# Gathers issued two steps ahead into 22 buffers, and a block's maxima computed in three parts from one step sooner

## The chip, the cores and the metric

The kernel runs on one core of a Trainium2 chip. The metric is the device time of one execution in microseconds (us). The engines are named as in the profile: PE is TensorE, DVE is VectorE, ACT is ScalarE, POOL is GpSimd, and SP is SyncE, which here only issues transfers. PEld is PE's loading of weights.

## The reference

A graph layer with attention over relations, followed by a residual and two layer norms. There are 3125 nodes of 128 features, 100000 edges sorted by destination, five edge types (relations), and eight heads of 16 features. Cut to what matters:

```python
for r in range(R):                                   # 5 relations
    mask = edge_types == r
    q = einsum('eh,khd->ekd', x[dst], W_Q[r]); k = ...x[src], W_K[r]; v = ...x[src], W_V[r]
    logits = (q * k).sum(-1) / 4 + attn_bias[r]
    masked = where(mask, logits, -1e9)
    max_v = segment_max(masked, dst)                 # per node, relation, head
    exp_l = where(mask, exp(masked - max_v[dst]), 0)
    attn = exp_l / (segment_sum(exp_l, dst)[dst] + 1e-12)
    out += segment_sum(attn[:, :, None] * v, dst)
h = out @ out_proj_w.T + out_proj_b + x
y = x + layer_norm(h) * gamma + beta
result = layer_norm(y)
```

Every node therefore needs the largest logit of its edges, for each relation and head, before any of its edges can be weighted.

## The kernel before, in words

A first stage (until about 125 us in the profile) builds tables in HBM: keys and values of every node and relation (`kv_d`, 256 floats a row), queries (`q_d`), and indices of the edges.

The main stage is a software pipeline written out by hand. The edges are cut into 196 groups of 512, and the loop `for k in range(-4, ...)` is over *steps*. The order in which the calls stand in the loop is the order of each engine's instructions; every engine runs its own list in order and waits for others through semaphores. In step k these things happen, each on a group of its own:

- POOL gathers keys and values for a later group: `gather` (L699), four indirect transfers per group, into one of `KVB` buffers that are used in turn. A gather may start when the buffer's earlier group has been weighted (`weigh`, L939).
- PE spreads the maxima to the edges of a group that is due (`spread_m`, L921), sums weighted values (`sums`, L973, L975, L982), and spreads queries to the edges of the next group (`spread_q`, L804).
- DVE weights values (`weigh`, L939), subtracts maxima (`less_max`, L930), normalises a finished group (`norm`, L994 to L997), computes the logits of group k (`logits`: `prod` L817, `lg` L818), and marks destinations (`spot`, L795). There is one L817 per step, so these cut the trace into steps.
- ACT does exponentials, copies, and one-hot places (`places`, L959, L962). SP issues the other loads and stores, among them the logits' store to `lg_d` (L823).

The nodes are cut into 25 blocks of 128. A block needs its maxima once all of its edges have logits. Call F the step in which the last group that can hold an edge of the block has its logits (`full_step[b]` in the code; about every eighth step). Then:

- In step F+1, POOL loads the logits of the block's nodes, 64 edges for each, by one indirect transfer (`maxima_load`, L830, tile `ell`), behind that step's gather.
- In steps F+3 and F+4, at the end of DVE's list for the step, `maxima` finds the maxima: first `by_head` (ACT, L845) and `mine` (L853), then for each relation of the part a mask `shut` (L863), then for all of the part's relations at once a sum `wl` (L868) and a reduction into `mx` (L874). The first part takes three relations (`RH`), the second takes two, and ends with six small instructions that make three bfloat16 pieces (L879 to L889).
- In step F+5 the pieces are stored, in F+6 they are fetched for the first group of the block, and in step F+8 (`ready[b]`, `LAG` = 8) that group is weighted. The 25th block is smaller and does its maxima in one part.

Two other sequences share the engines with this. Every block's queries are made in steps of their own by PE (`queries`, L725, tile `prq`, one PSUM buffer), and the second product can start only after DVE's `remainder` (L735) has read the first. The finished nodes of a block pass through `project`, `residual`, `roots` and `norms`.

In the code, step F+3 is `ready[b] - 5` and F+4 is `ready[b] - 4`. A group is weighted 16 to 19 steps after its logits, 19 for all groups from number 22 on, counted from 0.

Of the kernel before, what the change touches and what calls it, by code (L numbers as in the profile page):

```python
# [21 lines left out]
R = 5  # L22
# [26 lines left out]
RH = 3  # L49
# [1 line left out]
LW = HEADS + 1  # L51
PW = H + HEADS
FAR = 4000
AHEAD = 3
LAG = 8
LAG_H = 7
HALVED = 0
# [3 lines left out]
SPAD = 5  # L61
XG = range(3, 16, 3)
QB = 3
KVB = 23
HELD = 21
KVA = 9

# [66 lines left out]
def windowed_path(  # L134
# [554 lines left out]
    ps = ctx.enter_context(tc.tile_pool(name="ps", bufs=2, space=PSUM))  # L689
    buffers(i for i in range(KVB) if i not in at_once)  # L690
    hold = ctx.enter_context(tc.tile_pool(name="hold", bufs=HELD))
    flow = ctx.enter_context(tc.tile_pool(name="flow", bufs=2))
    late_flow = ctx.enter_context(tc.tile_pool(name="late_flow", bufs=2))
    def gather(g):
        if g in XG:
            return
        kv = kvs_[g % KVB]
        for t in range(T):
# [61 lines left out]
    def turn_x(g):  # L760
        xe = kvs_[g % KVB][:, :, H:]
        tx = ps.tile([P, T, P], F32, name="tx", tag="me")
# [27 lines left out]
    def put_kv(g, t0):  # L790
        nc.scalar.copy(kvs_[g % KVB][:, t0 : t0 + 2, :], live.pop(("pk", g, t0)))

# [21 lines left out]
    def logits(g):  # L814
        kv, lg = kvs_[g % KVB], live["lg", g]
        prod = flow.tile([P, T, H], F32, name="prod", bufs=1)
# [20 lines left out]
    def maxima(b, c0, c1):  # L837

        whole = MB[b][2] is None
        nh = HEADS if whole else HEADS // 2  # L840
        if c0 == 0:
            ell = live.pop(("ell", b))
            by_head = ps.tile([P, HEADS, D], F32, name="by_head", bufs=1)[:, :nh]
            if whole:
                nc.scalar.copy(by_head, ell[:, :, :HEADS].rearrange("p s k -> p k s"))  # L845
            else:
                for h in range(2):
                    at = slice(h * P // 2, (h + 1) * P // 2)
                    nc.scalar.copy(
                        by_head[at], ell[at, :, h * nh : (h + 1) * nh].rearrange("p s k -> p k s")  # L850
                    )
            mine = late_flow.tile([P, D], F32, name="mine", bufs=1)
            nc.vector.scalar_tensor_tensor(  # L853
                mine, slot, deg[:, b : b + 1], ell[:, :, HEADS], op0=ALU.is_lt, op1=ALU.mult
            )
            mx = late_flow.tile([P, R, HEADS], F32, name="mx", bufs=1)
            mx = mx.rearrange("p r k -> p (r k)")[:, : R * nh].rearrange("p (r k) -> p r k", k=nh)
            live["max", b] = by_head, mine, mx
        by_head, mine, mx = live["max", b]
        n = c1 - c0  # L860
        shut = late_flow.tile([P, R, D], F32, name="shut", bufs=1)
        for r in range(c0, c1):
            nc.vector.tensor_scalar(  # L863
                shut[:, r - c0, :], mine, float(r + 1), -BIG, op0=ALU.not_equal, op1=ALU.mult
            )
        wl = late_flow.tile([P, RH * HEADS, D], F32, name="wl", tag="wl", bufs=1)
        wl = wl[:, : n * nh].rearrange("p (r k) s -> p r k s", k=nh)
        nc.vector.tensor_tensor(  # L868
            wl,
            by_head[:, None].to_broadcast([P, n, nh, D]),  # L870
            shut[:, :n, None, :].to_broadcast([P, n, nh, D]),
            op=ALU.add,
        )
        nc.vector.tensor_reduce(mx[:, c0:c1], wl, AX.X, ALU.max)  # L874
        if c1 < R:
            return
        live.pop(("max", b))
        bias = bias4 if whole else bias_h
        nc.vector.tensor_tensor(mx, mx, bias, op=ALU.add)  # L879
        nc.vector.scalar_tensor_tensor(mx, mx, NEG4, bias, op0=ALU.max, op1=ALU.subtract)  # L880
        m3 = late_flow.tile([P, R, 2, 3, HEADS // 2], BF16, name="m3")
        if whole:
            mxs = mx.rearrange("p r (h k) -> p r h k", h=2)
        else:
            m3, mxs = m3[:, :, :1], mx[:, :, None, :]
        nc.vector.tensor_copy(m3[:, :, :, 0, :], mxs)
        nc.vector.tensor_tensor(mxs, mxs, m3[:, :, :, 0, :], op=ALU.subtract)
        nc.vector.tensor_copy(m3[:, :, :, 1, :], mxs)
        nc.vector.tensor_tensor(m3[:, :, :, 2, :], mxs, m3[:, :, :, 1, :], op=ALU.subtract)  # L889
        live["m3", b] = m3  # L890
# [45 lines left out]
    def weigh(g):  # L936
        wv, kv = late_flow.tile([P, T, PW], F32, name="wv"), kvs_[g % KVB]
        live["wv", g] = wv
# [149 lines left out]
    ready = [full_step[b] + lag(b) for b in range(NM)]  # L1088


    at_k, k = {}, 0
    for v in range(NGR):
        k = max(k + 1, ready[block_of(v, MEND)])
# [30 lines left out]
    for k in range(-4, root_at[NT] + 2):  # L1124
        v, g = v_at.get(k), group_at.get(k)
        q_step = {k - f: b for b, f in enumerate(q_from) if b >= QB and -2 <= k - f <= 5}

        if k >= 0 and k + 3 in group_at:
            fetch_keys(group_at[k + 3])
            fetch_q(group_at[k + 3])  # L1130
        if -2 in q_step:
            fetch_x("xq", q_step[-2])
        for b in range(NT):
            if done_at[b] - 1 == k:
                fetch_x("xr", b)
            if norm_at[b + 1] + 1 == k:
                store_z(b)
        for b in range(NM):
            if ready[b] - 3 == k:
                store_m(b)  # L1140
        if 5 in q_step:
            store_q(q_step[5])
        for u in range(NGR):
            if max(at_k[u] - 3, ready[block_of(u, MEND)] - 2) == k:
                fetch_m(u)
        for u in XG:
            if x_at[u] - 2 == k:
                fetch_types(u)

        while gathered < NGR - 1 and step_of[gathered + 1] <= k + (AHEAD if k < final - 16 else 1):  # L1150
            gathered += 1
            gather(gathered)
        for b in range(NM):
            if full_step[b] + 1 == k:
                maxima_load(b)

        for u in XG:
            if x_at[u] + 2 == k:
                put_kv(u, 0)
                put_kv(u, 2)  # L1160
        for b in range(NT):
            if done_at[b] + 1 == k:
                residual(b)
        if v_at.get(k - 4) is not None:
            by_node(v_at[k - 4])
        if v_at.get(k - 2) is not None:
            carry(v_at[k - 2])
        if 1 in q_step:
            turned(q_step[1])
        if 3 in q_step or 4 in q_step:  # L1170
            second_part()
        if 2 in q_step or 3 in q_step:
            first_part()

        if v_at.get(k + 1) is not None:
            spread_m(v_at[k + 1], 8 if k + 1 in group_at else 12)
        if v_at.get(k - 1) is not None or v_at.get(k - 3) is not None:
            sums(v_at.get(k - 1), v_at.get(k - 3))
        if k + 1 in group_at:
            spread_q(group_at[k + 1])  # L1180

        if v is not None:
            weigh(v)
        if v_at.get(k + 1) is not None:
            less_max(v_at[k + 1])
            exps(v_at[k + 1])
        if v is not None:
            weights(v)
        if k + 1 in group_at:
            types(group_at[k + 1])  # L1190
        if v_at.get(k - 2) is not None:
            norm(v_at[k - 2])
        if g is not None:
            logits(g)
            store_logits(g)
        if k + 2 in group_at:
            spot(group_at[k + 2])
        if v_at.get(k + 1) is not None:
            places(v_at[k + 1], 2 if k >= final - 1 else 0)
        if 3 in q_step or 4 in q_step:  # L1200
            third_part()
        if 2 in q_step or 3 in q_step:
            remainder()
        for b in range(NM):
            whole = MB[b][2] is None
            if ready[b] - 5 == k and whole:
                maxima(b, 0, RH)
            if ready[b] - 4 == k:
                maxima(b, RH if whole else 0, R)
        for b in range(NT):  # L1210
            if done_at[b] == k:
                project(b)
        for b in range(NT + 1):
            if root_at[b] == k:
                roots(b)
            if norm_at[b] == k:
                norms(b)
        for u in XG:
            if x_at[u] == k:
                turn_x(u)  # L1220
                by_relation(u)
            if x_at[u] + 1 == k:
                products(u, 0)
                products(u, 2)
        if 0 in q_step:
            turn_q(q_step[0])
        if 1 in q_step:
            queries(q_step[1], 0, RH)
        if 2 in q_step:
            queries(q_step[2], RH, R)  # L1230
# [505 lines left out]
```

## Time and profile before

| | |
|---|---|
| time, three runs | 1659.51, 1664.48 (median), 1679.92 us |
| profiled execution, its own time | 1665.2 us |
| its span, first to last instruction | 1663.5 us |
| mean granted TensorE clock | 0.724 of full speed |
| PE busy | 1043.0 us (63%) |
| DVE busy | 945.4 us (57%) |
| POOL busy | 796.5 us (48%) |
| ACT busy | 638.7 us (38%) |

The span is cut in two: up to the first logits at 146.7 us, and the pipeline from there. Groups 30 to 185 took 7.32 us per step in the mean, but the steps are far from equal, and it is the single steps that have to be read. No engine is busy all the time, and the chain of work that ended last passes from PE to DVE and back.

### The profile page before, as it was taken

Reading aid. Unit: us, or ns where it says so; the run is one execution under the profiler, and the core shown is the slowest. Engines: PE = TensorE matmul, PEld = TensorE weight load, DVE = VectorE, ACT = ScalarE, POOL = GpSimd, SP = SyncE. Lnnn points to the kernel's source line nnn. Section 1 sums busy time; section 2 is a strip of 40 time slices with the busy share of each in tenths; the row PEclk is TensorE's granted clock in tenths of the full one; section 3 lists DMA queues with packets and bytes.
Section 4 is the critical chain, followed back from the end, with each engine's and each line's share of the span. In section 5 each row is a group of like instructions: output and inputs, shape, how many; then the busy total and the mean of one; then the engine's idle time right before and its main releaser. Section 6 shows DMA issues by size and latency. Waiting matters only on the chain.

```text
span 1663.5 us, 26129 instructions
## 1 busy us (share of the span) xinstructions
PE 1043.0 (63%) x7746; PEld 790.5 (48%) x7746; DVE 945.4 (57%) x2536; ACT 638.7 (38%) x2258; POOL 796.5 (48%) x901
## 2 busy tenths in 40 slices
PE   6774836356566666665666666666566655665676
PEld 2443624245454444554554554555445544454564
DVE  3452626455564665556466555657555564564686
ACT  1450103144344444434445443444344343334344
POOL 6345061645465545545645554555455455445400
PEclk8885967677676767667676766777666776666878
DMA  6683343445455544544545454555445444444400
GB/s 161 232 309 105 72 134 80 108 124 137 101 135 126 132 110 121 137 109 118 144 118 129 126 137 107 137 131 131 108 120 139 109 122 120 107 118 108 102 16 15
DMA packets 181946, 203.66 MB, mean 122 GB/s; under 512 B 83943, under 2 KB 146819, under 8 KB 181676
## 3 DMA queue, kind: packets, MB, share of 16 engines
q0 software_dynamic: 40576, 112.08, 23.4%
q1 hardware_dynamic: 136790, 85.12, 21.9%
q10 hardware_dynamic: 4430, 4.71, 1.1%
q8 instruction: 64, 1.05, 0.3%
q14 instruction: 86, 0.70, 0.1%
HBM read 166.51 MB, written 35.28 MB: 121 GB/s over the span
## 4 chain that ended last, share of the span: by engine, by line
PE 29%; DVE 28%; issue 19%; another core or an unknown queue 10%; ACT 5%; DMA 2%; SPq 1%; DVEq 0%; ACTq 0%; POOL 0%
PE pp L973 9%; PE qe L804 4%; PE me L921 4%; DVE wl L868 4%; DVE mx L874 4%; DVE prod L817 4%; PE pk L782 3%; DVE wv L939 3%; DVE lg L818 2%; PE pp L975 2%; PE pr L404 2%; ACT at L959 2%; DVE hot L795 2%; PE prq L725 1%
## 5 line engine op out<-in xcount | busy, mean ns | idle before, releaser
L699 POOL DMA_INDIRECT kv<-kv_d,idx x764 | 724.5, 948 | 587.9 <-DVE den L994 346.6
L973 PE MATMUL pp<-wv,at 128*125 128x136 f32 x1568 | 392.7, 385 | 43.3 <-issue 34.1
L973 PEld LDWEIGHTS pp<-wv,at 128*125 128x125 f32 x1568 | 295.7, 256 | 122.4 <-issue 116.0
L804 PE MATMUL qe<-qw,hot 125*128 125x128 bf16 x2352 | 229.9, 256 | 87.7 <-issue 77.6
L921 PE MATMUL me<-mw,hot 125*128 125x64 bf16 (+1 forms) x2352 | 145.3, 217 | 217.6 <-issue 115.2
L804 PEld LDWEIGHTS <-hot 125*128 125x128 bf16 x2352 | 203.3, 125 | 99.6 <-issue 86.3
L921 PEld LDWEIGHTS <-hot 125*128 125x128 bf16 x2352 | 126.6, 113 | 253.5 <-issue 197.0
L934 ACT ACTIVATE me<-me 128x32 f32<-128x32 f32 x196 | 35.7, 182 | 542.0 <-DVE me L930 409.5
L959 ACT ACTIVATE at<-row_at,nkey 128x125 f32<-128x125 f32 x744 | 237.6, 398 | 0.0
L930 DVE TENSOR_TENSOR me<-lg,me 128x32 f32<-128x32 f32 x196 | 37.7, 193 | 348.6 <-remote 195.6
L939 DVE TENSOR_TENSOR wv<-kv,me 128x512 f32<-128x512 f32 x196 | 133.0, 679 | 104.0 <-remote 63.2
L817 DVE TENSOR_TENSOR prod<-kv,qe 128x512 f32<-128x512 f32 x196 | 132.9, 678 | 43.2 <-PE qe L804 25.7
L818 DVE TENSOR_REDUCE lg<-prod 128x32 f32<-128x512 f32 x196 | 134.5, 686 | 6.8
L975 PE MATMUL pp<-pt,carried 125*5 125x136 f32 x390 | 101.4, 350 | 57.8 <-ACT pt L988 27.4
L962 ACT ACTIVATE at<-at 128x500 f32<-128x500 f32 (+1 forms) x196 | 117.3, 599 | 6.2
L725 PE MATMUL prq<-wq,xTq 128*128 128x384 f32 (+1 forms) x88 | 52.7, 693 | 92.9 <-DVE hot L795 61.1
L1007 ACT COPY oT<-pp 128x25 f32 x196 | 33.7, 172 | 180.6 <-PE me L921 72.8
L830 POOL DMA_INDIRECT ell<-lg_d,start_i x25 | 23.6, 944 | 154.3 <-DMA lg_d<-lg 62.0
L782 PE MATMUL pk<-wkv,xm 128*128 128x256 f32 x200 | 62.9, 448 | 50.3 <-issue 46.3
L868 DVE TENSOR_TENSOR wl<-by_head,shut 128x1536 f32<-128x1536 f32 (+2 forms) x49 | 73.1, 1491 | 33.7 <-PE pk L782 25.6
L982 PEld LDWEIGHTS pp<-rsum,o 125*128 125x128 f32 x392 | 83.6, 257 | 14.0 <-issue 13.3
L982 PE MATMUL pp<-rsum,o 125*128 125x25 f32 x392 | 74.2, 270 | 12.8 <-issue 8.2
(191 smaller groups left out, 1199.5 us busy)
## 6 DMA issues: line engine op xcount, KB each, us to landing
kt<-key_d SPq DMA_DIRECT2D x196, 128.0 KB
qw<-q_d SPq DMA_DIRECT2D x196, 96.0 KB
kv_d<-kvs SPq DMA_DIRECT2D x24, 640.0 KB
kv<-kv_d,idx POOLq DMA_INDIRECT x764
q_d<-q SPq DMA_DIRECT2D x22, 480.0 KB
lg_d<-lg SPq DMA_DIRECT2D x196, 18.0 KB
mw<-m_d SPq DMA_DIRECT2D x196, 6.0 KB
xr<-in_x SPq DMA_DIRECT2D x24, 64.0 KB
```

The costliest lines, as they stand in the source:

```text
L699: nc.gpsimd.indirect_dma_start(out=kv[:, t, :], out_offset=None, in_=kv_d[:, :], in_offset=bass.IndirectOffsetOnAxis(ap=idx[:, t, g : g + ...
L804: nc.tensor.matmul(qe[:, t, :], hot[:, t, :], qw[:WR, s, :], start=(s == 0), stop=(s == 2))
L817: nc.vector.tensor_tensor(prod, kv[:, :, :H], live.pop(("qe", g)), op=ALU.mult)
L818: nc.vector.tensor_reduce(lg[:, :, :HEADS], prod.rearrange("p t (k d) -> p t k d", d=HD), AX.X, ALU.add)
L868: nc.vector.tensor_tensor(wl, by_head[:, None].to_broadcast([P, n, nh, D]), shut[:, :n, None, :].to_broadcast([P, n, nh, D]), op=ALU.add,)
L921: nc.tensor.matmul(me[:, t], hot[:, t, :], mw[:WR, None, :, s, :].to_broadcast([WR, times, 2, HEADS // 2]), start=(s == 0), stop=(s == 2),)
L939: nc.vector.tensor_tensor(wv[:, :, :H].rearrange("p t (k d) -> p t k d", d=HD), kv[:, :, H:].rearrange("p t (k d) -> p t k d", d=HD), live ...
L959: nc.scalar.activation(at[:, t, :], row_at[:, :WR], AF.Abs, bias=nkey[:, t, g : g + 1], scale=1.0)
L962: nc.scalar.activation(at[:, on_dve:], at[:, on_dve:], AF.Relu, bias=1.0, scale=-1.0)
L973: nc.tensor.matmul(pp, at[:, t, :], wv[:, t, :], start=(t == 0), stop=(t == T - 1))
L975: nc.tensor.matmul(pp[:R], carried[:WR, g, :], live.pop(("pt", g - 1)), start=False, stop=False,)
L982: nc.tensor.matmul(op, live.pop(("o5", done)), rsum[:WR], start=True, stop=True)
```

## The change

`AHEAD` goes from 3 to 2: a group's four gathers stand one step later in POOL's list. `KVB` goes from 23 to 22: there is one buffer of keys and values fewer. A whole block's maxima are computed in three calls, of two, two and one relations, in steps F+2, F+3 and F+4. The loads, the stores, `LAG` and the steps F+5 to F+8 stay where they are.

```diff
-AHEAD = 3
+AHEAD = 2
...
-KVB = 23
+KVB = 22
...
         for b in range(NM):
             whole = MB[b][2] is None
+            if ready[b] - 6 == k and whole:
+                maxima(b, 0, 2)
             if ready[b] - 5 == k and whole:
-                maxima(b, 0, RH)
+                maxima(b, 2, 4)
             if ready[b] - 4 == k:
-                maxima(b, RH if whole else 0, R)
+                maxima(b, 4 if whole else 0, R)
```

The loop that issues the gathers is the same in both:

```python
while gathered < NGR - 1 and step_of[gathered + 1] <= k + (AHEAD if k < final - 16 else 1):
    gathered += 1
    gather(gathered)
```

## Prediction

> **What bounds the kernel now.** I read the page first. No engine is full, and section 4 gives PE and DVE nearly equal shares of the chain that ended last. A mean over 200 steps says nothing here, so I cut the trace at the 196 instructions of L817, one per step, and looked at DVE's busy time in each step of a block.
>
> ```profile
> PE 1043.0 (63%) x7746; PEld 790.5 (48%) x7746; DVE 945.4 (57%) x2536; ACT 638.7 (38%) x2258; POOL 796.5 (48%) x901
> ...
> PE 29%; DVE 28%; issue 19%; another core or an unknown queue 10%; ACT 5%; DMA 2%; SPq 1%; DVEq 0%; ACTq 0%; POOL 0%
> ```
>
> The table of windows, for the steps F+2 to F+5 of the twelfth block (F = 97), shows what the page hides. Columns: window, length, busy time and count of PE, PEld, DVE, ACT and POOL, granted clock, DMA share, GB/s.
>
> ```profile
> 877.40:887.56 10.16, 6.07 (x41) 4.97 (x41) 4.46 (x17) 4.06 (x17) 5.84 (x7) 0.67 0.53 137
> 887.56:894.80 7.24, 6.06 (x60) 5.10 (x60) 6.96 (x14) 3.22 (x12) 3.46 (x5) 0.79 0.50 114
> 894.80:901.80 7.00, 3.77 (x36) 3.06 (x32) 6.62 (x19) 2.88 (x12) 3.77 (x5) 0.68 0.51 118
> 901.80:907.85 6.05, 3.87 (x23) 2.87 (x23) 3.37 (x11) 3.28 (x13) 4.53 (x6) 0.52 0.58 122
> ```
>
> In F+3 and F+4 DVE is busy for 6.96 of 7.24 us and 6.62 of 7.00 us: it sets the pace, and these are the steps that hold the maxima. In F+2 it is busy for 4.46 of 10.16 us. All blocks look like this. Over the 17 blocks from the fifth on, F+3 lasts 7.40 us in the mean and F+4 7.01 us, with DVE busy for 6.97 and 6.63.
>
> The waits over the steady part (300 to 1580 us) show what DVE's lateness costs, and where DVE itself waits.
>
> ```profile
> PE prq L725 <- DVE hot L795: 61.1, 13, 5.6
> PE prq L725 <- DVE rem L735: 30.0, 6, 5.6
> ...
> DVE me L930 <- remote: 195.6, 24, 19.1
> DVE wv L939 <- remote: 63.2, 21, 11.9
> ```
>
> The first two rows are one wait per block, 91.1 us over 19: PE has nothing to do in F+4 and F+5 until DVE, behind its maxima, reaches the `remainder` (L735) that frees the buffer of `prq`. The last two rows are about one long wait of DVE per block, and most of them lie in F+2. There PE itself issues slowly: in the twelfth block the last four products of L973 before 885.8 us follow each other with pauses of 0.35 to 1.8 us. The profile names no releaser for these pauses. So in F+2 DVE waits for PE, and in F+3 and F+4 PE waits for DVE.
>
> **The change part by part.** *The maxima.* Durations by form:
>
> ```profile
> L868 DVE TENSOR_TENSOR wl<-by_head,shut 128x1536 f32<-128x1536 f32 x24 | 42.2, 1758 | 32.4 <-PE pk L782 25.6 <-ACT by_head L845 4.7 <-ACT at L962 1.1
> L874 DVE TENSOR_REDUCE mx<-wl 128x24 f32<-128x1536 f32 x24 | 42.1, 1753 | 0.8
> L868 DVE TENSOR_TENSOR wl<-by_head,shut 128x1024 f32<-128x1024 f32 x24 | 29.4, 1225 | 0.8
> L874 DVE TENSOR_REDUCE mx<-wl 128x16 f32<-128x1024 f32 x24 | 29.3, 1220 | 0.8
> L853 DVE SCALAR_TENSOR_TENSOR mine<-slot,deg,ell 128x64 f32<-128x64 f32 x25 | 8.2, 328 | 0.0
> ```
>
> 512 elements fewer are 0.53 us fewer, so a part of one relation takes 1.225 - 0.533 = 0.69 us for each of its two large instructions; L817, also 128x512, has 0.68. A third `shut` adds 0.11 us to two.
>
> - F+3 loses `mine` (0.33), one `shut` (0.11), and 0.53 in each of L868 and L874: 1.5 us.
> - F+4 loses one `shut` (0.11) and 0.53 twice: 1.2 us.
> - F+2 gains `mine` (0.33), two `shut` (0.29 in the timeline), 1.225, 1.220 and some 0.05 of gaps: 3.1 us.
>
> So 2.7 us leave two steps that DVE bounds, 3.1 us enter a step in which DVE waits, and 0.4 us per block is the price of the extra pair of instructions. What hides the 3.1 us is DVE's wait for PE: the new instructions stand behind that step's `hot`, ahead of the next step's `wv` and `me`, where the wait is. I took DVE's idle time in F+2 block by block for the first 23 blocks. In 19 of them it is between 3.3 and 19.2 us. In the fifteenth it is 2.0, so 1.1 us shows. In the 7th, 13th and 20th the slow stretch of PE fell into F+1, the idle time is 0.2 to 0.4 us, and all but that shows; the block then gains -0.1 us. Sum: 19 x 2.7 + 1.6 - 0.3 = 52.6 us.
>
> *Can PE follow?* PE is idle for 5.1 us in the mean over F+3 and F+4, more than 2.7. But in 8 of the 17 blocks F+3 ran at a clock of 0.57 or less, and PE was busy for some 6.6 us; DVE will then need 7.4 - 1.5 = 5.9, and 0.7 us stay with PE. For about 11 of 23 blocks that is 8 us. I take 52.6 - 8 = 44.6. Bounds from the rows: were F+3 and F+4 at 0.50 in every block, PE would need 6.6 and 3.5 x 0.86 / 0.50 = 6.0 us, and the saving is 0.8 + 1.0 in 19 blocks, 34 us. The other way, F+5 runs at 0.52 right after PE's long wait. At F+4's mean clock of 0.86, its 3.6 busy us, run at a mean of 0.58, would be 2.4, and 1.2 x 19 = 23 us more are gained. I take neither, because F+7, where PE is busy nearly throughout, was at 0.50 in 10 of the 17 blocks.
>
> The Trainium skill speaks here ("TensorE: Matmul & The Clock Gate", section "HAM oscillation — how this bites in real kernels"): idle gaps of PE over some 3.4 us put it back to half speed. The row beside it: waits of 4.8 us for `prq` and 0.52 in the step after. By the rule these waits, cut to some 2 us, would leave F+5 at full speed, and its busy time would halve: an estimate of 1.8 us x 19, some 34 us more than my sum. No row here shows that step without the wait.
>
> *`ell` and `by_head` a step sooner.* DVE's `mine` and ACT's `by_head` (1.06 us) now need `ell` at the end of F+2. Adding up the packets of the gathers' queue, `ell` lands 1.7 to 3.0 us after its issue ends. That is before the end of `hot` in F+2 in 20 of 23 blocks, by 1 to 18 us; in three it is 0.7 to 1.4 us after, in front of idle time of 13 us or more. So nothing shows: 0, at most 3 us. On ACT the copy stands ahead of the next step's `oT` and `pt`, as it does now a step later; its waiters on PE cost 3.1 us in all.
>
> *The gathers.* A gather waits for the weighting of its buffer's old group. Before, in step k, group k+3 waits for group k+3-23 = k-20; after, group k+2 waits for k+2-22 = k-20. It is the same group, weighted in step k-1, so POOL's list keeps its times with a different group in each place: one group's lead of one step is lost, and nothing is issued later than its buffer was free. `ell` stands behind one gather fewer in the count, and behind the same wait. By the packets a group lands 1.6 us after its fourth issue ends, and from group 23 to 181 at least 15 us before its L817. With the next group's landing in its place the smallest margin is 8.4 us (group 67), then 10.1. Cost 0. Without that cover, a late group costs up to 4 x 1.25 = 5.0 us of issues.
>
> A rule against the change stands in the Trainium skill ("SBUF — State Buffer", the note on the "DVE blocks DMA" trap): a DVE instruction in a two-port mode locks POOL out while it writes descriptors, and F+2 is where POOL is busiest (5.84 us above). The row decides: a gather that began under L868 (at 1359.13 us) took 0.95 us, against a median of 0.946 for all.
>
> *Elsewhere.* The lists of PE and SP keep their order. The first block's new part stands ahead of `xm` (L771) in step 10, where DVE waits 10.4 us anyway. The 24th block's last part is 1.2 us shorter, in the tail; I count 0.
>
> The profiled execution took 1665.2 us, 0.7 over the median of the three runs. 1665.2 - 44.6 = 1620.6: I predict 1621.
>
> **The rivals.** *The gain is given back in PE's slow stretches.* For it: DVE's wait in F+2 and PE's `PE me L921 <- issue: 115.2` (72 times) have no releaser in the profile. If such a stretch ends at a time set from outside and not after a fixed amount of work, arriving 2.7 us earlier only waits longer. Against it: the stretches come at the same steps of each block, as if the list set them off. Half the gain would go: 1665 - 26 = 1639. If they move into F+1 in most blocks, F+2 covers nothing and the time is 1665.
>
> *The gathers' lead decides, and it is slower.* With two steps, a group's margin is the length of two to three steps less 6.6 us (5.0 of issues, 1.6 to land). Three steps in a row last as little as 8.8 us where DVE catches up (2.9 each). If keys and values come late from there on, L817 waits in each block for up to 5.0 us: 19 x 5.0 - 52.6 = +42, 1707 us. It begins to decide when 8.4 us of margin are gone. Against it: DVE's waits for `kv` at L817 sum to 0.5 us in the whole profile.
>
> *PE bounds F+3 and F+4 at once.* That is the lower bound above: 1665 - 34 = 1631.
>
> **How the numbers follow.** A difference of 2%, 33 us here, is about what a measurement of this kernel can tell from no change. The forecast with its own range, 1598 (the clock's 23 us more) to 1631, has 0.52; a gain that is partly or wholly given back, 1631 to 1665, 0.32; a small loss 0.05; the gathers' lead 0.11. Faster by over 2% means under 1631: 0.52. Slower by over 2%: 0.11. The rest, 0.37, is within. The range reaches from 1598 to 1664 and leaves the losses out.
>
> **What would show it.** Right: L868 as 48 of 128x1024 and 24 of 128x512, the first of a block in F+2; F+3 and F+4 at about 5.9 to 6.6 and 5.8 us; PE's wait for `prq` down from 4.8 to some 2 us a block; no wait of L817 for `kv`. Wrong: F+3 and F+4 shorter, but F+6 to F+9 longer by as much; F+2 longer by 3 us; or `DVE prod L817 <- DMA kv` among the waits.

## The result, and the profile after

| | before | after |
|---|---|---|
| time, median of 4 runs | 1668.98 us (1659.51 to 1679.92) | 1623.51 us (1617.89 to 1627.16) |
| ratio | | 0.9722 [0.965, 0.9795] |
| profiled execution / its span | 1665.2 / 1663.5 us | 1617.9 / 1616.1 us |
| first logits to step 30 | 146.7 to 378.1 us | 148.7 to 377.7 us |
| steps 30 to 185 | 1134.0 us, 7.32 a step | 1092.6 us, 7.05 a step |
| last logits to the end | 79.9 us | 75.3 us |

The change makes the kernel faster by 2.8%: 1623.51 us, where 1621 were forecast. The ratios here and below leave out the runs of a second, slower state (over 1.5% above the same kernel's fastest), while medians and ranges hold all runs. Of the 47.4 us between the two spans, 41.4 lie in steps 30 to 185 and 4.6 behind the last logits.

First the by-form view of the kernel after, L868 and its neighbours (count, busy time in us, mean ns, idle time before it).

```profile
L868 DVE TENSOR_TENSOR wl<-by_head,shut 128x1024 f32<-128x1024 f32 x48 | 58.8, 1225 | 34.3 <-PE pk L782 18.3 <-issue 8.4 <-ACT at L962 5.2
...
L868 DVE TENSOR_TENSOR wl<-by_head,shut 128x512 f32<-128x512 f32 x24 | 16.6, 691 | 0.8
L874 DVE TENSOR_REDUCE mx<-wl 128x8 f32<-128x512 f32 x24 | 16.5, 686 | 0.8
L853 DVE SCALAR_TENSOR_TENSOR mine<-slot,deg,ell 128x64 f32<-128x64 f32 x25 | 8.1, 325 | 3.3 <-DMA ell<-lg_d,start_i 3.3
```

There are 48 and 24 of the two shapes, and a part of one relation costs 0.691 and 0.686 us. `mine` waits 3.3 us for `ell` in the whole profile. The table of windows, again for F+2 to F+5 of the twelfth block (length, then busy time and count of PE, PEld, DVE, ACT, POOL, then clock, DMA share, GB/s):

```profile
868.80:878.30 9.50, 3.60 (x25) 2.40 (x22) 7.29 (x22) 3.87 (x15) 5.18 (x7) 0.77 0.51 131
878.30:886.60 8.30, 6.62 (x62) 5.22 (x62) 5.52 (x13) 2.63 (x12) 5.84 (x7) 0.85 0.58 135
886.60:892.50 5.90, 3.61 (x24) 2.75 (x21) 5.52 (x18) 2.88 (x12) 1.70 (x3) 0.58 0.48 110
892.50:902.20 9.70, 6.57 (x56) 5.43 (x57) 3.40 (x11) 3.32 (x13) 7.20 (x8) 0.68 0.54 129
```

F+2 now holds 7.29 us of DVE instead of 4.46 and is no longer than it was. F+4 fell from 7.00 to 5.90 us. But F+3 is longer than before, with DVE idle for 2.8 us of it, and so is F+5. The means over the 17 blocks from the fifth on say the same, with DVE's busy time in brackets:

| | F+0 | F+1 | F+2 | F+3 | F+4 | F+5 | F+6 | F+7 | sum |
|---|---|---|---|---|---|---|---|---|---|
| before | 6.58 | 6.77 | 10.69 [4.25] | 7.40 [6.97] | 7.01 [6.63] | 5.58 | 7.53 | 7.24 | 58.8 |
| after | 4.55 | 7.17 | 10.01 [7.20] | 6.60 [5.52] | 6.62 [5.55] | 9.59 | 4.42 | 7.84 | 56.8 |

The waits of the kernel after, over its steady part (300 to 1540 us):

```profile
DVE me L930 <- remote: 270.5, 42, 15.9
POOL kv L699 <- DVE den L994: 249.8, 63, 10.9
...
PE me L921 <- issue: 102.2, 91, 6.6
...
PE prq L725 <- DVE rem L735: 41.4, 11, 7.0
...
PE prq L725 <- DVE hot L795: 3.7, 4, 1.5
```

PE's wait for `prq` is 41.4 us, with 3.7 more behind `hot`, where it was 91.1. PE's pauses without a releaser are still there. To count them I add up every gap over 0.25 us between two successive products of the same line and tile that the profile puts down to no releaser (`issue`): 218.5 us in the whole profile before, 217.1 after, and 135.7 and 133.2 in steps 30 to 185. They moved. In F+3 and F+4 there were 0.1 us of them per block before and 1.6 after; in F+6 2.0 before and 0.2 after.

### The profile page after: what moved, and what is told of

It reads as the page before. It is cut to its first block, busy times and chain, and to the rows that moved or that the text cites. A ratio compares the mean times of both kernels' runs of the same rounds, so it can differ in the third digit from the quotient of the medians.

```text
span 1616.1 us, 26179 instructions
## 1 busy us (share of the span) xinstructions
PE 1026.6 (64%) x7746; PEld 779.1 (48%) x7746; DVE 954.9 (59%) x2584; ACT 640.8 (40%) x2258; POOL 796.4 (49%) x901
## 3 DMA queue, kind: packets, MB, share of 16 engines
q8 instruction: 64, 1.05, 0.3%
## 4 chain that ended last, share of the span: by engine, by line
PE 31%; DVE 23%; issue 19%; another core or an unknown queue 13%; ACT 4%; DMA 3%; POOL 2%; DVEq 0%; SPq 0%; ACTq 0%; POOLq 0%
PE pp L973 10%; PE qe L804 5%; PE me L921 4%; DVE prod L817 4%; PE pk L782 3%; DVE wv L939 3%; PE pp L975 3%; DVE lg L818 3%; DVE wl L868 2%; PE pr L404 2%; DVE mx L874 2%; PE prq L725 2%; POOL kv L699 1%; DVE hot L795 1%
## 5 line engine op out<-in xcount | busy, mean ns | idle before, releaser
L973 PE MATMUL pp<-wv,at 128*125 128x136 f32 x1568 | 387.7, 379 | 44.9 <-issue 39.1
L973 PEld LDWEIGHTS pp<-wv,at 128*125 128x125 f32 x1568 | 290.4, 251 | 124.0 <-issue 118.6
L921 PE MATMUL me<-mw,hot 125*128 125x64 bf16 (+1 forms) x2352 | 147.2, 216 | 242.6 <-issue 102.2
L804 PE MATMUL qe<-qw,hot 125*128 125x128 bf16 x2352 | 231.3, 255 | 93.4 <-issue 78.5
L930 DVE TENSOR_TENSOR me<-lg,me 128x32 f32<-128x32 f32 x196 | 37.7, 192 | 388.6 <-remote 270.5
L921 PEld LDWEIGHTS <-hot 125*128 125x128 bf16 x2352 | 127.7, 113 | 278.7 <-issue 250.0
L817 DVE TENSOR_TENSOR prod<-kv,qe 128x512 f32<-128x512 f32 x196 | 132.8, 677 | 44.9 <-PE qe L804 24.5
L975 PE MATMUL pp<-pt,carried 125*5 125x136 f32 x390 | 97.7, 340 | 42.2 <-ACT pt L988 23.2
L830 POOL DMA_INDIRECT ell<-lg_d,start_i x25 | 23.6, 946 | 172.1 <-DMA kt<-key_d 62.4
L868 DVE TENSOR_TENSOR wl<-by_head,shut 128x1024 f32<-128x1024 f32 (+2 forms) x73 | 76.9, 1053 | 35.6 <-PE pk L782 18.3
L982 PEld LDWEIGHTS pp<-rsum,o 125*128 125x128 f32 x392 | 81.7, 251 | 20.3 <-issue 19.9
L725 PE MATMUL prq<-wq,xTq 128*128 128x384 f32 (+1 forms) x88 | 48.5, 639 | 49.9 <-DVE rem L735 41.9
```

The costliest lines, as they stand in the source:

```text
L804: nc.tensor.matmul(qe[:, t, :], hot[:, t, :], qw[:WR, s, :], start=(s == 0), stop=(s == 2))
L817: nc.vector.tensor_tensor(prod, kv[:, :, :H], live.pop(("qe", g)), op=ALU.mult)
L921: nc.tensor.matmul(me[:, t], hot[:, t, :], mw[:WR, None, :, s, :].to_broadcast([WR, times, 2, HEADS // 2]), start=(s == 0), stop=(s == 2),)
L973: nc.tensor.matmul(pp, at[:, t, :], wv[:, t, :], start=(t == 0), stop=(t == T - 1))
L975: nc.tensor.matmul(pp[:R], carried[:WR, g, :], live.pop(("pt", g - 1)), start=False, stop=False,)
L982: nc.tensor.matmul(op, live.pop(("o5", done)), rsum[:WR], start=True, stop=True)
```

## The experiments

The runs fell on three chips, four on each, always beside runs of the kernel before on the same chip. I call the chip of the result above the first; the record does not name it, so it may be the same as the fourth. On the second and the third the kernel before takes 1214 us, on the fourth 1666 us, like on the first. This difference between chips turned out to hold the answer. The expectations of the first four runs were written before it was known, and those of the last four with the times of the second and third chip in mind.

### The parts of the change, on the second chip (before: 1214.22 us)

*The maxima alone.* The kernel after, with the gathers as they were:

```diff
-AHEAD = 2
+AHEAD = 3
-KVB = 22
+KVB = 23
```

> The kernel before with only the maxima in three parts from F+2 on; gathers three steps ahead into 23 buffers as before. Theory (all of the gain is DVE work moved out of F+3 and F+4 into DVE's wait in F+2, the gathers are neutral): 1615 to 1632 us, ratio 0.97 to 0.98, the same as the whole change. Rival (the later gathers carry part of the gain, by giving other transfers and PE's slow stretches more room): 1640 us or more, ratio 0.985 or more.

Measured: 1259.89 us (1257.11 to 1262.71), ratio 1.0385 [1.0348, 1.0421]. Slower, so the theory is wrong here. The rival's ratio is met and its reason is not, as the next run shows.

*The gathers alone.* The kernel before with `AHEAD = 2` and `KVB = 22`.

> The kernel before with only AHEAD = 2 and 22 buffers; maxima in two parts as before. Theory (POOL's list keeps its times, margin of 8.4 us or more): within 0.7% of before, 1660 to 1676 us, and no wait of L817 for kv in the steady part. Rival that the gathers carry part of the gain: 1650 us or less. Rival that the shorter lead costs: 1680 us or more.

Measured: 1215.74 us (1210.88 to 1221.01), ratio 1.0005 [0.9973, 1.0036]. In time the gathers cost nothing and bring nothing here. But one sign that the theory excluded is there, in the steady part (260 to 1140 us):

```profile
DVE prod L817 <- DMA kv<-kv_d,idx: 9.3, 6, 3.7
```

Keys and values come late in six places. In the whole profile it is 12.4 us, against 2.8 with the maxima alone, where the gathers keep their three steps. The time does not show it.

*Two parts, one step sooner.* The kernel before, with its parts of three and two relations in F+2 and F+3:

```diff
-            if ready[b] - 5 == k and whole:
+            if ready[b] - 6 == k and whole:
                 maxima(b, 0, RH)
-            if ready[b] - 4 == k:
+            if ready[b] - (5 if whole else 4) == k:
                 maxima(b, RH if whole else 0, R)
```

> The kernel before with its two parts of three and two relations moved one step sooner, to F+2 and F+3; F+4 has no maxima. It tells 'sooner' from 'in smaller pieces'. Theory (DVE's wait in F+2 covers what is put there): F+3 falls by about 0.45 us to 7.0, F+4 from 7.0 to what PE needs, 4.2 to 6.1; F+2 hardly grows where its idle time was over 4.6 us. 1665 - 19 x 2.4 - 8 gives 1605 to 1630 us. Rival (the even spread is what counts, since 4.6 us in one step are not covered): F+2 grows by 3 us or more, 1640 us or more.

Measured: 1267.47 us, ratio 1.0435 [1.0379, 1.0491]. This is the rival's sign: F+2 lasts 11.54 us in the mean, against 4.69 with the gathers alone.

*One relation per part.* The kernel after, in which each of a whole block's three parts computes one relation (0, 2 and 4) and fills the others' maxima with zeros, so 2 of the 5 relations are left out:

```diff
-        n = c1 - c0
+        n = 1
+        if c1 - c0 > 1 and whole:
+            nc.vector.memset(mx[:, c0 + 1 : c1], 0.0)
+        n = n if whole else c1 - c0
...
-        for r in range(c0, c1):
+        for r in range(c0, c0 + n):
...
-        nc.vector.tensor_reduce(mx[:, c0:c1], wl, AX.X, ALU.max)
+        nc.vector.tensor_reduce(mx[:, c0 : c0 + n], wl, AX.X, ALU.max)
```

> The changed kernel with the maxima of one relation found in each of the three parts (relations 0, 2 and 4) and the other two set to zero: 1.2 us of DVE less in F+2 and in F+3 each. It measures what the maxima still cost. Theory (after the change PE and its slow stretches set most of the pace, DVE still some of F+3): 1.2 us of F+3 saved in about half of the blocks, and of F+2 in those with no idle time left: 10 to 30 us under the changed kernel, 1594 to 1614 us. Rival (the maxima are fully hidden now): the same time as the changed kernel within 5 us. Rival (DVE still bounds F+2 to F+4 throughout): 2.4 x 23 = 55 us less, 1569 us.

Measured: 1218.17 us, ratio 1.003 [1.0006, 1.0054]. That is 41.7 us under the maxima alone, between the theory's 10 to 30 and the second rival's 55.

Why the sign turns is seen in the windows. The gathers alone, F+2 to F+4 of the twelfth block:

```profile
635.80:640.60 4.80, 3.91 (x50) 3.26 (x49) 4.34 (x17) 3.93 (x17) 3.58 (x5) 1.00 0.92 227
640.60:647.80 7.20, 4.31 (x52) 3.19 (x50) 6.92 (x14) 3.19 (x12) 5.64 (x6) 1.00 0.83 191
647.80:654.80 7.00, 3.78 (x36) 3.08 (x32) 6.62 (x19) 2.88 (x12) 5.21 (x6) 0.68 0.55 143
```

F+3 and F+4 are as on the first chip, set by DVE. F+2 is not: it lasts 4.80 us, of which DVE is busy for 4.34. There is no cover. PE makes no pause here: the gaps counted as above sum to 0 in the whole profile, and so they do in all eight runs on the second and the third chip. So the first part's 3.1 us lengthen F+2, and more comes on top. The waits with the maxima alone (260 to 1140 us):

```profile
DVE mine L853 <- DMA ell<-lg_d,start_i: 46.3, 18, 3.9
POOL kv L699 <- DVE den L994: 38.9, 54, 1.2
...
DVE wl L868 <- ACT by_head L845: 11.1, 21, 1.5
```

`ell` is issued in F+1, and here it lands after DVE wants it: 46.3 / 18 = 2.6 us in each of 18 blocks, and 0.5 more for `by_head`. Mean F+2 goes from 4.69 (gathers alone) to 10.40 us, while F+3 and F+4 together go from 14.70 to 11.59. The net is 2.6 us a block.

Can a block make that up later? POOL's list speaks against it. In the kernel with the gathers alone, a gather and the gap behind it take 0.95 + 0.30 us. A block of eight steps has 33 such issues, 41.3 us, and lasts 42.0 us. With the gathers alone, waits of POOL for `den` (the weighting's chain) are 0.6 us; with the maxima alone they are 38.9. A late weighting holds POOL, and POOL has 0.7 us a block to spare. With one relation per part F+2 is still 9.61 us, but F+3 is 4.54 and F+4 5.99, and the block lasts 42.8: a long F+2 costs little as long as the next two steps give it back. That POOL's list is what keeps a block from catching up is read from these sums. The runs with more room for POOL, which would have tested it, fell on the other kind of chip.

### What the loss consists of, on the third chip (before: 1214.09 us)

*The changed kernel itself.*

> The changed kernel as it is, beside the kernel before on the chip of the experiments, where the kernel before took 1214 us and not 1665. New theory: the gain needs DVE's wait in F+2, and that wait came from pauses between PE's instructions, which the traces of this second chip do not have (12 us of them against 230). So here the changed kernel is slower: the maxima alone cost 3.9% and the gathers alone nothing, so 1.03 to 1.045 times before, some 1255 to 1268 us. Rival (the two parts of the change help each other, and the gathers alone or the maxima alone do not show it): ratio 1.0 or less.

Measured: 1256.48 us, ratio 1.0331 [1.0255, 1.0406]. This is as expected, and like the maxima alone. (By the count of pauses above, the 230 and 12 us of the expectation are 218.5 and 0.) F+2 to F+4 of the twelfth block:

```profile
653.10:664.20 11.10, 7.02 (x59) 6.23 (x59) 7.27 (x22) 3.91 (x15) 8.06 (x10) 0.65 0.69 163
664.20:669.80 5.60, 5.60 (x38) 4.57 (x36) 5.43 (x14) 2.53 (x12) 3.75 (x5) 0.51 0.62 159
669.80:675.70 5.90, 3.13 (x38) 2.31 (x35) 5.52 (x18) 2.87 (x12) 3.80 (x5) 1.00 0.47 139
```

F+3 and F+4 are shorter by 1.6 and 1.1 us than with the gathers alone: the saving that was forecast is there, 2.7 us. F+2 has grown by 6.3.

*`ell` ahead of the gathers.* In step F+1 the loop of gathers is moved behind the load of the logits:

```diff
-        while gathered < NGR - 1 and step_of[gathered + 1] <= ...:
-            gathered += 1
-            gather(gathered)
         for b in range(NM):
             if full_step[b] + 1 == k:
                 maxima_load(b)
+        while gathered < NGR - 1 and step_of[gathered + 1] <= ...:
+            gathered += 1
+            gather(gathered)
```

> The changed kernel with maxima_load placed ahead of step F+1's gather in POOL's list, so that ell is issued up to 5 us sooner. On this chip the run with the maxima alone waited 46 us for ell at L853 (18 times 2.6) and 11 us for by_head at L868. Theory (on a chip without the pauses the price is these waits, about 2.6 us a block, plus 0.4 us more DVE work a block and 3.1 us no longer covered against 2.7 saved): 18 x 2.6 = 47 us come back, 1205 to 1225 us, ratio 0.995 to 1.01. Rival (the price is DVE's work in F+2 itself, and the wait for ell only shows where DVE would wait for PE anyway): within 10 us of the changed kernel.

Measured: 1265.44 us, ratio 1.0423 [1.0346, 1.05]: not faster than the changed kernel. Its waits (260 to 1140 us):

```profile
DVE mine L853 <- DMA ell<-lg_d,start_i: 32.1, 16, 2.9
DVE prod L817 <- DMA kv<-kv_d,idx: 16.3, 18, 3.8
```

The wait for `ell` fell only from 45.3 to 32.1 us, and the gathers that stand behind it now come late at L817, where the changed kernel waited for 0.3 us. So the place of `ell` in POOL's list is not the price; what is gained there is paid by the gathers. POOL's own waits right before the load (L830) rose from 41.8 to 58.4 us: the load, moved ahead, mostly waits longer. The theory's gain of 47 us did not come. Whether the wait for `ell` is the price is not settled, since most of it stayed.

*PE late on purpose.* Into the kernel before and into the changed one I put 20 products of 128x256 ahead of L921 in step F+3 of 23 blocks; their result is overwritten. They lengthen F+2 by making PE, and through it DVE's next `me`, late: a cover like the one that the first chip has and this one lacks, though made of work and not of pauses.

```diff
+        for _ in range(late):
+            nc.tensor.matmul(
+                me.rearrange("p t n h k -> p (t n h k)")[:, :256], ones, wkv[:, 0].rearrange("h s c -> h (s c)"),
+                start=True, stop=True,
+            )
...
+                20 if k - 3 in full_step[:NF - 1] else 0,
```

> The kernel before with 20 idle products of 128x256 (about 0.38 us each, 7.6 us) put ahead of L921 in step F+3 of the first 23 blocks: an artificial lateness of PE in the place where the first chip's PE paused. F+2 to F+3 grow by up to 7.6 us: 1214 + 23 x 4 to 7 = 1300 to 1375 us. It is the reference for the next run.

Measured: 1373.30 us (1368.94 to 1389.96), ratio 1.1301 [1.1189, 1.1413].

> The changed kernel with the same 20 products in step F+3. Theory (what decides the sign is whether DVE waits for PE after F+2's logits): with the wait put back, part one and the wait for ell lie under it, and F+3 and F+4 are shorter: 15 to 55 us faster than the kernel before with the same products. Rival (the gain on the first chip came from something else, such as its transfers): it stays 30 to 50 us slower than that kernel, as without the products.

Measured: 1312.71 us (1310.67 to 1327.88), ratio 1.0833 [1.0726, 1.0939]. Against the kernel before with the same late PE that is 1.0833 / 1.1301 = 0.959, or 4.1% less; the two profiled spans differ by 1367.5 - 1312.9 = 54.6 us, at the upper end of the 15 to 55 us expected. F+2 to F+4 of the twelfth block, first before, then changed:

```profile
700.10:713.40 13.30, 13.30 (x81) 11.18 (x80) 4.41 (x16) 2.86 (x12) 10.25 (x11) 0.89 0.62 163
713.40:720.80 7.40, 4.90 (x61) 3.93 (x61) 7.10 (x14) 3.22 (x12) 2.26 (x3) 1.00 0.39 93
720.80:727.80 7.00, 3.69 (x36) 2.98 (x33) 6.62 (x19) 2.88 (x12) 3.77 (x5) 0.70 0.46 118
```

```profile
679.40:693.00 13.60, 13.60 (x79) 11.49 (x78) 7.35 (x22) 3.61 (x12) 10.40 (x11) 0.84 0.59 160
693.00:698.60 5.60, 5.22 (x63) 4.09 (x62) 5.43 (x13) 2.53 (x12) 1.32 (x2) 1.00 0.37 94
698.60:704.50 5.90, 2.80 (x36) 2.19 (x32) 5.52 (x18) 2.88 (x12) 3.80 (x5) 0.97 0.59 134
```

PE is busy for all of F+2 in both. DVE's 2.9 us more in F+2 all but disappear in it (means of F+2 12.68 and 12.89 us), and F+3 and F+4 together last 27.11 - 12.68 = 14.43 and 24.47 - 12.89 = 11.58 us in the mean. With the cover the same change gains 4.1%; without it, on the same chip, it loses 3.3%. `ell` is waited for here too (44.6 us), inside the cover.

### Room in the buffers, on the fourth chip (before: 1665.57 us)

A gather may start when its buffer has been weighted, 20 steps back in both kernels (23 - 3 and 22 - 2). Three of these four kernels have one step more of this room, one has two.

> The changed kernel with KVB 23 instead of 22: a buffer comes free one step before its gather is due. Theory (the loss on a chip without PE's pauses comes in two pieces, F+2 longer by 5.6 us and no room for POOL to make it up, since its 33 issues of 1.25 us fill 41.3 of 42.0 us per block): POOL's waits for the weighting (34.7 us before a gather, in the steady part) fall under 10 us, F+5 to F+1 get no shorter than POOL's issues allow, and 15 to 30 us of the 42 us of loss come back: 1226 to 1241 us. Rival (DVE's own list in F+2 sets the end, POOL's waits are only a sign of it): POOL's waits fall as well, and the time stays within 8 us of 1256.

> The changed kernel with KVB 24: two steps of room. Theory: POOL's waits for the weighting are gone and POOL can issue through F+2 without a stop; the time is 1216 to 1236 us and not over that with KVB 23. Rival: 1256 again, within 8 us.

> The kernel before with LAG 7 instead of 8: its two parts of the maxima (three and two relations) stand in F+2 and F+3, and unlike in the kernel with only those two parts moved, which took 1267 us, the stores, fetches and the weighting also come one step sooner, so that every buffer comes free one step sooner. Theory: the long F+2 (11.5 us there) stays, POOL's waits for the weighting (53.9 us there) fall under 15, and with one step less of pipeline (about 5 us) the time is 1225 to 1245. Rival (F+2 alone sets the price): 1267 less the one step, 1257 to 1265.

> The kernel before with KVB 24 instead of 23. If POOL's issues bound it there (41.3 us of 42.0 per block), room in the buffers can bring at most 0.7 us in each of some 20 blocks, 14 us: 1200 to 1214 us. Rival (it was already waiting for buffers): more than 14 us are gained, under 1200.

| kernel | edit | room | time, us | ratio to before |
|---|---|---|---|---|
| before | | 20 | 1665.57 | 1 |
| before, one buffer more | `KVB` 23 to 24 | 21 | 1738.11 (1735.07 to 1743.25) | 1.0435 [1.0393, 1.0477] |
| changed, one buffer more | `KVB` 22 to 23 | 21 | 1697.03 (1679.57 to 1701.92) | 1.0173 [1.0088, 1.0258] |
| changed, two buffers more | `KVB` 22 to 24 | 22 | 1775.53 (1770.58 to 1779.26) | 1.0661 [1.0612, 1.0711] |
| before, all one step sooner | `LAG` 8 to 7 | 21 | 1729.71 (1719.45 to 1742.08) | 1.0415 [1.0349, 1.0482] |

None of the expectations holds. They were made for a chip on which POOL's issues bound the kernel, and this is not one. What the runs tell instead is of more use.

First, the change is in this table a second time: the two kernels with one buffer more differ by the whole change, at a room of 21 instead of 20, and the changed one is faster by 1738.11 - 1697.03 = 41.1 us, 2.4%. In the means F+3 and F+4 together fall from 14.42 to 11.78 us, by 2.64; F+2 goes from 18.89 to 20.31, and F+5 and F+6 trade time as on the first chip (5.63 to 9.40, 7.47 to 4.60). A block is shorter by 1.9 us.

Second, more room costs: 72.5 us for the first buffer in the kernel before, and 78.5 us from one to two in the changed one. The first buffer lengthens F+2 by 8.2 us, from the 10.69 of the first chip's profile to 18.89, of which F+0 and F+1 give back 4.2. The second lengthens F+2 by 2.6 and F+3 by 1.5 us. The changed kernel with one buffer more, F+2 to F+4 of the twelfth block:

```profile
891.90:913.30 21.40, 7.54 (x54) 5.48 (x53) 7.21 (x21) 4.47 (x16) 13.23 (x14) 0.53 0.44 115
913.30:919.00 5.70, 5.44 (x47) 4.21 (x46) 5.53 (x14) 2.63 (x12) 0.42 (x1) 0.68 0.35 76
919.00:924.90 5.90, 2.75 (x35) 2.14 (x31) 5.52 (x19) 2.88 (x12) 3.80 (x5) 0.91 0.53 137
```

No engine but POOL is busy for more than 7.6 of the 21.4 us. The same stretch in the timeline, POOL and then PE (start, duration, instruction, idle time before it):

```profile
888.45 0.94 POOL L830 DMA_INDIRECT ell<-lg_d,start_i  x1 [6.73 <-DMA lg_d<-lg]
889.70 0.95 POOL L699 DMA_INDIRECT kv<-kv_d,idx  x1 [0.30 <-issue]
...
908.45 0.94 POOL L699 DMA_INDIRECT kv<-kv_d,idx  x1 [0.30 <-issue]
```

```profile
904.72 0.27 PE L804 MATMUL qe<-qw,hot 125*128 125x128 bf16 x1 [1.20 <-issue]
906.82 0.27 PE L804 MATMUL qe<-qw,hot 125*128 125x128 bf16 x1 [1.83 <-issue]
908.22 0.27 PE L804 MATMUL qe<-qw,hot 125*128 125x128 bf16 x1 [1.13 <-issue]
909.62 0.26 PE L804 MATMUL qe<-qw,hot 125*128 125x128 bf16 x1 [1.14 <-issue]
911.02 0.27 PE L804 MATMUL qe<-qw,hot 125*128 125x128 bf16 x1 [1.13 <-issue]
...
912.45 0.82 PE L804 MATMUL qe<-qw,hot 125*128 125x128 bf16 x6 [0.44 <-issue]
```

With room, POOL arrives at the load of `ell` early and has to wait there for the logits' store (6.7 us here). The gathers queue up behind it, and when the store has landed POOL issues 17 in a row, 888 to 909 us. From 898 us on, PE's products come 1.4 to 2.8 us apart, and some 3 us after the last issue they come at their own pace again. The unbroken run that holds `ell` has 9.2 issues in the mean of the 17 blocks after, 10.2 before, 15.6 and 16.1 with one buffer more (before, changed), and 20.1 with two; mean F+2 is 10.0, 10.7, 18.9, 20.3 and 22.9 us. With all one step sooner it is 14.2 issues and 13.9 us, but there the maxima moved too. In the changed kernel with one buffer more, pauses fill 111 of the 315 us of runs of 17 issues, and 6 of the 207 us of runs of 4. In the changed kernel itself the tie is looser: they fill 24 of the 325 us of runs of 4.

That more room lengthens F+2 on this chip is shown, since `KVB` is all that differs between the kernels compared (23 and 24 before, 23 and 24 changed). That the runs of gathers are what slows PE is read from where the pauses lie, and not shown by a run that changes them alone. Why PE slows is open: on the second and third chip there are runs of up to 231 issues and no pause without a releaser at all.

## Why the prediction was right, point by point

- *The bound.* DVE did set F+3 and F+4. Their medians over the 17 blocks fell from 7.45 and 7.00 to 6.14 and 5.91 us (forecast 5.9 to 6.6, and 5.8).
- *The sizes.* DVE's busy time changed by +2.95, -1.45 and -1.08 us in F+2, F+3 and F+4; forecast +3.1, -1.5, -1.2. A part of one relation was 0.691 and 0.686 us for a forecast of 0.69.
- *The cover.* F+2 did not grow (10.69 to 10.01 us) while it took in 2.95 us of DVE. The pair with late PE shows that such a cover decides the sign: -4.1% with it, +3.3% without, on one chip.
- *2.7 us in each of 19 blocks.* Nearly right in the medians (-1.3 and -1.1 us), wrong in the means: F+3 and F+4 lost only 0.80 + 0.39 = 1.2 us, and 1.6 us of PE's pauses a block now fall into them. F+2 lost another 0.7, which was not forecast, so that F+2 to F+4 together give 1.9 of the block's 2.0 us. The other five steps shifted by much more (-2.0 in F+0, -3.1 in F+6, +4.0 in F+5) and all but cancel. This is the rival of the slow stretches, in part: they moved when everything around them moved, but did not eat the gain. The forecast of 44.6 us for 23 blocks is 1.9 a block. That it was met so closely is in part luck, since terms that it had wrong, here and in the next two points, cancel. The replica with one buffer more, most of whose pauses stay in F+2, has the 2.64 us in the means.
- *The tail.* Counted as 0, it gave 4.6 us (79.9 to 75.3). On the other chips the changed kernel's tail is 74.9 to 75.4 us too. With the gathers alone it is 80.2 us and with the maxima alone 74.9, so there it comes from the maxima. This term was too small.
- *Can PE follow?* Not in 9 of the 17 blocks. There F+3 lasts 6.1 to 8.3 us, 7.4 in the mean, where DVE is busy for 5.5, and in seven of them DVE waits 1.1 to 2.6 us for PE at L930. In the other 8 it lasts 5.6 to 5.9. The forecast had PE too late in about half of the blocks, and by 0.7 us instead of 1.9. (Before, F+3 ran at 0.57 or less in 9 of the 17 blocks, not 8.) How much of that is the clock and how much the moved pauses cannot be separated. Neither bound came true.
- *PE's wait for `prq`.* 45.1 us over 19 blocks, 2.4 a block; forecast some 2, from 4.8. The mean is right and the picture behind it is not. In six of the 17 blocks a wait of 3.5 to 4.5 us is left, and F+5 runs at a clock of 0.50 to 0.65. In eight it is gone or at most 0.8 us, because PE itself is late, and F+5 runs at 0.66 to 0.79.
- *The clock.* In the mean F+5 went from 0.58 to 0.66, not to 1, and F+6 fell from 0.75 to 0.57; the whole profile went from 0.724 to 0.731. The rule on idle gaps that I set beside the sum ("TensorE: Matmul & The Clock Gate" of the Trainium skill) is neither confirmed nor refuted by this. Its estimate of 34 us assumed waits of some 2 us in every block; where the wait went, PE's lateness came in its place, and F+5 still did not run at full speed. From a mean clock of 0.58 the estimate would have been 3.6 x 0.42 x 19 = 29 us. The trace before did have rows of F+5 without the wait: in the 20th and 21st block it falls into F+6, and F+5 ran at 1.00.
- *`ell`.* `mine` waits 3.3 us; forecast 0 to 3. On the chips without PE's pauses the changed kernel waits 44 to 46 us, also with late PE, where F+2 lasts 12.9 us. So the estimate holds for this chip, and a long F+2 alone does not explain why.
- *The gathers.* 0.3 us at L817 for `kv` on the first chip. On the second the gathers alone moved the time by 0.05%, so the rival of the lost lead, 5.0 us in each block, is refuted. L817 did wait for `kv` there, for 9.3 us in six places; without a trace of the kernel before on that chip it is open how much of that is new. (Three steps in a row last 9.0 us at least in the trace before, not 8.8.) That the room stays at 20 was treated as a reason to count nothing; the fourth chip shows that a step of it has the highest price of all, some 75 us.

What the prediction did not ask is whether its cover belongs to the kernel. It took a wait that no releaser explained as given, and was right on this chip and, with one buffer more in both kernels, on the fourth. On the two chips without PE's pauses the same change costs 3.3% (third chip), and its maxima alone 3.9% (second). What stays open: how the gain on the first chip splits between maxima and gathers, since the gathers alone ran only on a chip without the pauses (the lines of F+3 and F+4 speak for the maxima); and whether less room, `KVB` 21 with `AHEAD` 2, would shorten F+2 further there. The runs point to that version, and it was not run.

## What to carry to other kernels

Before work is moved under an idle time, ask who ends that idle time; where the profile names no releaser, the cover may be the chip's and not the kernel's, and the forecast should say that it holds for chips like the profiled one. The same edit can be tested for this by putting the cover in by hand. And a queue that runs ahead as far as its buffers let it is not free: on the fourth chip one more buffer made this kernel 4% slower, and with it the gathers came in longer runs behind one load.

## What the runs showed of the hardware

- The kernel before takes 1214 us on the second and third chip, and 1666 to 1669 on the fourth and the first, with mean granted TensorE clocks of 0.80 to 0.82 and 0.71 to 0.72. The clock is not all of it: PE's pauses without a releaser are 218.5 us in the profile of the kernel before on the first chip, and none in any of the eight profiles on the second and third.
- An indirect gather of 128 rows holds POOL for 0.95 us, and the next starts 0.30 us later, on all chips. 33 of them in a block of eight steps are 41.3 us; with the gathers alone, on the second chip, a block lasted 42.0 us.
